# A graph-attention and hypergraph kernel on one core: D^-1 on a path of its own, and a new order of copies, LayerNorm and leaky steps

## The chip, the cores and the metric

The kernel runs on one core of a Trainium2 chip. The metric is the device time of the core in microseconds (us), the median of several runs. Before the change it is 2611.13 us (3 runs, 2609.69 to 2614.38).

In what follows PE is TensorE (matmuls), DVE is VectorE, ACT is ScalarE, POOL is GpSimd and SP is SyncE, which issues nearly all transfers (DMAs). Each engine works through its own instructions in their order and waits for the others by semaphores.

## The reference

There are 128 graphs of 128 nodes with 512 features. Two layers follow each other; each is x = LayerNorm(x + f(x, adj)). Cut to what is computed:

```python
# layer 0: attention with 8 heads of 64 units
feats  = einsum('bnf,hfu->bhnu', X, W)
e_self, e_neigh = feats . a_self, feats . a_neigh
dense  = leaky_relu(e_self[..., :, None] + e_neigh[..., None, :], 0.2)
dense  = dense + -1e10 * (1.0 - A[:, None])
att    = softmax(dense, axis=-1)
x      = layernorm(x + relu(einsum('bhij,bhju->bhiu', att, feats) + b))

# layer 1: two hypergraph convolutions with a ReLU and a LayerNorm between them
H   = (adj != 0);  w = first row of adj
Dn  = 1 / sum_e H[c, e] w[e]      # 0 where the sum is not positive
Be  = 1 / sum_c H[c, e]
conv(x, W, b) = Dn * (H @ (Be * (H^T @ (x W^T)))) + b
x   = layernorm(x + conv(layer_norm(relu(conv(x, W1, b1))), W2, b2) + x)
```

D^-1 in the title is Dn: one number for each node of each graph.

## The kernel before

The kernel takes two graphs ("a pair") at a time, 64 pairs. Each pair goes through several planned periods of T = 38.6 us, and several pairs are in flight. Every step has a planned place, written as (periods after the pair's own start, us within the period). The steps of all pairs are sorted by that time, and this gives the order of the instructions on every engine. The planned times only set the order; nothing waits for a clock.

```python
T = 38.6
for p in range(PAIRS):
    if p > 1:
        todo.append((p * T, load, (p,)))
    if p:
        todo.append((p * T + 19.0, load_blocks, (p,)))
    for lag, time, fn, skip in steps:
        ...
            todo.append(((p + lag) * T + time + shift(p, lag, time), on_pair, (fn, p)))
...
    for _, fn, args in sorted(todo, key=lambda e: e[0]):
        fn(*args)
```

The matrix products are done with a scheme of seven block products in place of eight; it adds several products into one PSUM bank, "X", and needs copies of X between them. For the last dense product of a pair ("py") the products 1, 2, 6, 5, 7, 4, 3 stand at these times, and the copies 0, 1, 2 of X at the last three:

```python
chain("py", 3, (24.2, 29.4, 27.7, 32.9, 31.2, 35.35, 37.1, 26.2, 29.6, 33.1), weigh,
      QU, 1)

def copy(p, s, i):
    ...
    nc.scalar.copy(t[:, :n], s[kind, "X"][:, :n])
```

Product 4 (at 35.35) adds into X again and so has to wait for copy 2 (at 33.1). Product 3 (at 37.1) adds into the bank "W", which a sum on DVE (at 34.9) reads first.

The attention scores start with two small row vectors for each head, e_self and e_neigh. A feature tile ft holds them in its first two columns. The kernel gathers e_neigh, together with D^-1, in a small tile "columns", transposes it, writes it to memory and reads it back spread over all 128 partitions:

```python
@step(0, 11.0)
def nodes(p, s):
    ...                                        # dd = sum of w where adj is not 0
    dn = small.tile([P, 2], F32, tag="dn", name=f"dn_{p}")
    nc.vector.tensor_scalar(dn, dd, TINY, None, op0=ALU.max)
    nc.vector.reciprocal(dn, dn)
    nc.vector.scalar_tensor_tensor(
        columns[p % 2][:, B - CS:B - CS + 2], dd, 0.0, dn, op0=ALU.is_gt, op1=ALU.mult
    )

@step(1, 25.0)
def spread_rows(p, s):
    t = columns[p % 2]
    nc.vector.tensor_copy(
        t[:, B - 2 * H:].rearrange("p (g h) -> p g h", g=2), s["ft"][:, :, :, 1]
    )
    rows = work.tile([P, B], F32, tag="rows", name=f"rows_{p}")
    nc.vector.transpose(rows, t)
    ...
        nc.sync.dma_start(rd.rearrange("b c j -> (b c) j"), rows)

@step(1, 27.0)
def neighbours(p, s):
    s["nb"] = work.tile([P, 2, H * N], F32, tag="nb", name=f"nb_{p}")
    for g in range(2):
        spread(p, s, s["nb"][:, g, :], slice(2 + g * H, 2 + (g + 1) * H))
    s["dnb"] = work.tile([P, 2 * N], F32, tag="dnb", name=f"dnb_{p}")
    spread(p, s, s["dnb"], slice(0, 2))
```

nb then gets the mask (POOL), the leaky step with e_self as its bias (ACT), the maximum (DVE) and the exponential (ACT), for two graphs g and two halves q of the heads. In the loop below tm, tl and tx are the times of mask, leaky step and maximum:

```python
def masked(p, s, g, q):
    ...
    nc.gpsimd.tensor_tensor(
        t, t, neg[:, :, None, :].to_broadcast([P, NB, HH, B]), op=ALU.add
    )

def leaky(p, s, g, q):
    for h in range(q * HH, (q + 1) * HH):
        t = scores(p, s, g, h)
        nc.scalar.activation(t, t, AF.Prelu, bias=s["ft"][:, g, h, 0:1], alpha=SLOPE)

for (g, q), tm, (lag, tl), (lagx, tx), te, tt in (
    ((0, 0), 31.0, (1, 32.4), (1, 33.9), 2.7, 18.1), ((0, 1), 32.2, (1, 34.0), (1, 36.7), 4.6, 18.15),
    ((1, 0), 34.2, (1, 37.5), (2, 2.0), 7.8, 21.5), ((1, 1), 35.4, (2, 6.0), (2, 7.3), 7.9, 21.55),
):
    at(1, tm, masked, g, q)
    at(lag, tl, leaky, g, q)
    ...
```

In the same stretch of a period the pair before is at its first LayerNorm: rstds (a small DVE step "vea" and a power "rsa" on POOL), first_shift ("sh", DVE) and first_output (the scaled and shifted y, ACT). Its y feeds the products "pz", which ACT copies to zT, which feeds the products "ph":

```python
at(2, 32.7, rstds, "a")

@step(2, 34.95)
def first_shift(p, s):
    s["sh"] = small.tile([P, 2], F32, tag="sh", name=f"sh_{p}")
    nc.vector.scalar_tensor_tensor(
        s["sh"], s["mv", "a"][:, :, 0], -1.0, s["rs", "a"], op0=ALU.mult, op1=ALU.mult
    )

def first_output(p, s, g):
    t = s["y"][:, g, :]
    nc.scalar.activation(
        t, t, AF.Identity, bias=s["sh"][:, g:g + 1], scale=s["rs", "a"][:, g:g + 1]
    )

at(2, 35.7, first_output, 0)
at(2, 35.75, first_output, 1)
...
at(3, 0.0, propagate, 0)       # pz
at(3, 0.9, propagate, 1)
...
at(3, 1.1, z_evict, 0)         # zT
at(3, 2.0, z_evict, 1)
```

Two more parts are touched. r_evict multiplies the propagator R by dnb (DVE, at (1, 35.8)). load_blocks loads x and adj in blocks of 32 rows (tiles xb and ab), in four transfers each; ab is used by the step edges at (1, 3.4).

Of the kernel before, what the change touches and what calls it, by code (L numbers as in the profile page):

```python
# [8 lines left out]
F32 = mybir.dt.float32  # L9
AF = mybir.ActivationFunctionType  # L10
ALU = mybir.AluOpType
# [5 lines left out]
TINY = 1.1754944e-38  # L17
# [3 lines left out]
def kernel(  # L21
# [44 lines left out]
    nc = tc.nc  # L66
    G, N, F = x.shape
    P = 128
    DH = w1t.shape[1]
    H = 8  # L70
# [8 lines left out]
    B = 32  # L79
    NB = P // B  # L80

    const = ctx.enter_context(tc.tile_pool(name="const", bufs=1))
    work = ctx.enter_context(tc.tile_pool(name="work", bufs=1))
    small = ctx.enter_context(tc.tile_pool(name="small", bufs=4))
    dram = ctx.enter_context(tc.tile_pool(name="dram", bufs=3, space=bass.MemoryType.DRAM))
# [6 lines left out]
    st = {}  # L92
# [10 lines left out]
    def load_blocks(p):  # L103
        s = st[p]
        gs = slice(2 * p, 2 * p + 2)

        s["xb"] = work.tile([P, 2 * NB, P], F32, tag="xb", name=f"xb_{p}")
        rows = x[gs].rearrange("g (b n) (f c) -> f n (g b) c", b=NB, f=NB)
        for f in range(NB):
            nc.sync.dma_start(s["xb"][f * B:(f + 1) * B], rows[f])  # L110

        s["ab"] = work.tile([P, 2 * NB, B], F32, tag="ab", name=f"ab_{p}")
        rows = adj[gs].rearrange("g (b n) (f e) -> f n (g b) e", b=NB, f=NB)
        for f in range(NB):
            nc.sync.dma_start(s["ab"][f * B:(f + 1) * B], rows[f])

# [15 lines left out]
    for dst, i, j in ((w0_sb[:, 0], 0, 0), (w0_sb[:, 1], 1, 0), (w0_12, 0, 1), (w0_sb[:, 2], 1, 1)):  # L132
        raw = work.tile([P, KF // 2, QU], F32, tag=("eT", "nb", "sq", "hS")[2 * i + j], name=f"w0_raw{i}{j}")
        nc.sync.dma_start(
            raw, w0.rearrange("(p k) c -> p k c", k=KF)
            [:, i * KF // 2:(i + 1) * KF // 2, j * QU:(j + 1) * QU],
        )
        if (i, j) == (1, 0):
            load_blocks(0)
        w0_blocks.append((dst, raw.rearrange("p k (h u) -> p k h u", h=HH), j))  # L140

    def everywhere(ap, n, name):
# [36 lines left out]
    for i in range(2):  # L179
        t = const.tile([P, 2, H, UW + 1], F32, name=f"ft{i}")  # L180
        nc.gpsimd.memset(t[:, :, :, UW:], 1.0)
        fts.append(t)

    CS = 2 + 2 * H
    columns = []
    for i in range(2):
        t = const.tile([P, B], F32, name=f"columns{i}")
        nc.gpsimd.memset(t[:, :B - CS], 0.0)
        columns.append(t)

    def second_sums(eng, w, b12):

# [75 lines left out]
    def step(lag, time, skip_first=False):  # L268
        def keep(fn):
            steps.append((lag, time, fn, skip_first))  # L270
            return fn
        return keep

    def at(lag, time, fn, *args, skip_first=False):
        step(lag, time, skip_first)(lambda p, s: fn(p, s, *args))
# [28 lines left out]
    @step(0, 11.0)  # L304
    def nodes(p, s):

        a = s["a"]
        dd = small.tile([P, 2], F32, tag="dd", name=f"dd_{p}")
        w = s["w"]
        for g in range(2):  # L310
            nc.vector.scalar_tensor_tensor(
                w[:, g, :], a[:, g, :], 0.0, w[:, g, :], op0=ALU.not_equal, op1=ALU.mult,
                accum_out=dd[:, g:g + 1],
            )
        dn = small.tile([P, 2], F32, tag="dn", name=f"dn_{p}")
        nc.vector.tensor_scalar(dn, dd, TINY, None, op0=ALU.max)
        nc.vector.reciprocal(dn, dn)
        nc.vector.scalar_tensor_tensor(
            columns[p % 2][:, B - CS:B - CS + 2], dd, 0.0, dn, op0=ALU.is_gt, op1=ALU.mult
        )  # L320
    @step(0, 38.4)
    def mask(p, s):
        s["neg"] = work.tile([P, 2, N], F32, tag="neg", name=f"neg_{p}", bufs=2)
# [51 lines left out]
    @step(1, 35.8)  # L375
    def r_evict(p, s):
        s["R"] = work.tile([P, 2, N], F32, tag="R", name=f"R_{p}", bufs=3)
        nc.vector.tensor_tensor(
            s["R"].rearrange("p g (b n) -> p g b n", b=NB),
            s["pd"][:, :2 * N].rearrange("p (g b n) -> p g b n", g=2, b=NB),  # L380
            blocked(p, s["dnb"], 2).rearrange("p b g n -> p g b n"), op=ALU.mult,
        )


# [59 lines left out]
    @step(1, 25.0)  # L444
    def spread_rows(p, s):


        t = columns[p % 2]
        nc.vector.tensor_copy(
            t[:, B - 2 * H:].rearrange("p (g h) -> p g h", g=2), s["ft"][:, :, :, 1]  # L450
        )
        rows = work.tile([P, B], F32, tag="rows", name=f"rows_{p}")
        nc.vector.transpose(rows, t)
        shape = [B, NB, B] if p == 0 else [NB, B, B]
        rd = s["rd"] = dram.tile(shape, F32, tag="rd", name=f"rd_{p}")
        if p == 0:
            for b in range(NB):
                nc.sync.dma_start(rd[:, b, :], rows[b * B:(b + 1) * B])
        else:
            nc.sync.dma_start(rd.rearrange("b c j -> (b c) j"), rows)  # L460

    def spread(p, s, dst, rows):

        src = s["rd"]
        rows = slice(B - CS + rows.start, B - CS + rows.stop)
        if p == 0:
            src = src[rows].rearrange("c b j -> (c b j)")
        else:
            dst = dst.rearrange("p (b x) -> p b x", b=NB)
            src = src[:, rows, :].rearrange("b c j -> b (c j)")  # L470
        nc.sync.dma_start(dst, src.partition_broadcast(P))

    def blocked(p, t, n):

        dims = "p (c b j) -> p b c j" if p == 0 else "p (b c j) -> p b c j"
        return t.rearrange(dims, b=NB, c=n)

    @step(1, 27.0)
    def neighbours(p, s):
        s["nb"] = work.tile([P, 2, H * N], F32, tag="nb", name=f"nb_{p}")  # L480
        for g in range(2):
            spread(p, s, s["nb"][:, g, :], slice(2 + g * H, 2 + (g + 1) * H))
        s["dnb"] = work.tile([P, 2 * N], F32, tag="dnb", name=f"dnb_{p}")
        spread(p, s, s["dnb"], slice(0, 2))

    def scores(p, s, g, hs):
        return blocked(p, s["nb"][:, g, :], H)[:, :, hs, :]

# [62 lines left out]
                )  # L553

    for (g, q), tm, (lag, tl), (lagx, tx), te, tt in (
        ((0, 0), 31.0, (1, 32.4), (1, 33.9), 2.7, 18.1), ((0, 1), 32.2, (1, 34.0), (1, 36.7), 4.6, 18.15),
        ((1, 0), 34.2, (1, 37.5), (2, 2.0), 7.8, 21.5), ((1, 1), 35.4, (2, 6.0), (2, 7.3), 7.9, 21.55),
    ):
        at(1, tm, masked, g, q)
        at(lag, tl, leaky, g, q)  # L560
        at(lagx, tx, largest, g, q)
        at(2, te, exponential, g, q)
        at(2, tt, e_transpose, g, q, skip_first=True)
# [64 lines left out]

    at(2, 26.2, residual, 0)
    at(2, 30.7, residual, 1)  # L630
    at(2, 32.7, rstds, "a")

    @step(2, 34.95)
    def first_shift(p, s):
        s["sh"] = small.tile([P, 2], F32, tag="sh", name=f"sh_{p}")
        nc.vector.scalar_tensor_tensor(
            s["sh"], s["mv", "a"][:, :, 0], -1.0, s["rs", "a"], op0=ALU.mult, op1=ALU.mult
        )
# [4 lines left out]
            t, t, AF.Identity, bias=s["sh"][:, g:g + 1], scale=s["rs", "a"][:, g:g + 1]  # L643
        )

    at(2, 35.7, first_output, 0)
    at(2, 35.75, first_output, 1)

    def skip(p, s, g):

# [194 lines left out]
    def o_norm(p, s):  # L845
# [5 lines left out]
    T = 38.6  # L851
    todo = [
        (11.1, prepare_first, (0,)), (12.0, prepare_first, (1,)), (13.0, prepare_first_sums, ()),
        (65.0, prepare_output, ()), (71.4, prepare_output_sums, ()), (73.7, prepare_hidden, (0,)),
        (75.6, prepare_hidden, (1,)), (77.5, prepare_hidden, (2,)), (77.6, prepare_hidden, (3,)),
        (82.0, prepare_output_blocks, ()), (83.0, prepare_output_block_sums, ()),
    ]
# [4 lines left out]
    def shift(p, lag, time):  # L862

        if p == 0:
            if lag == 0:
                return 2.5 if time < 12.0 else 0.0
            if lag == 1 and 4.0 < time < 10.0:
                return -T + (6.8 if time < 6.0 else 8.0)
            if lag == 2 and time < 8.5:
                return -0.8 * time  # L870
        if p == 1 and lag == 1:
            if time < 4.0:
                return -6.0
            return -17.5 if time < 10.0 else -13.0 if time < 12.0 else -23.1 if time < 26.0 else 0.0
        return 0.0

    for p in range(PAIRS):
        if p > 1:
            todo.append((p * T, load, (p,)))
        if p:  # L880
            todo.append((p * T + 19.0, load_blocks, (p,)))
        for lag, time, fn, skip in steps:
            if p or not skip:
                todo.append(((p + lag) * T + time + shift(p, lag, time), on_pair, (fn, p)))
# [47 lines left out]
```

## Time and profile before

| | before |
|---|---|
| median of 3 runs | 2611.13 us |
| span of the profiled run | 2606.9 us |
| mean granted TensorE clock | 0.989 |
| mean DMA rate | 132 GB/s |
| first pz product | 89.6 us after the start |
| first to last pz product | 2469.0 us |

The page gives busy time and share of the span for each engine, and groups of instructions by line, engine and operation with their count and mean duration. "L295" is line 295 of the kernel; a tile's name stands without its buffer number, as in "py<-pyX", which is a copy from the bank X to a tile py. The waits say which engine's instruction stood idle and what ended the idle time. A timeline line has the start and the duration of one piece in us, engine, line, operation, output and inputs, shape, a count, and in brackets the idle time before it and what ended it.

### The profile page before, as it was taken

The numbers are of one execution on the slowest core, as the hardware profiler recorded it, in microseconds if no ns is written. First come the engines' busy times: TensorE is split into PE (matmuls) and PEld (weight loads), VectorE is DVE, ScalarE is ACT, GpSimd is POOL, SyncE is SP. The second block draws the span as 40 slices with busy tenths as digits, with TensorE's granted clock in tenths as the row PEclk, the third lists the DMA queues.
The fourth block names the chain that finished last, engine by engine and source line by source line (L and its number), as shares of the span: only waits on it lengthen the run. The fifth ranks groups of instructions, "written<-read, shape, count | busy, mean of one in ns | idle before, by whom it ended". The sixth has DMA issues, their size and how long they took to land.

```text
span 2606.9 us, 48113 instructions
## 1 busy us (share of the span) xinstructions
PE 2520.7 (97%) x16304; PEld 2274.7 (87%) x16304; DVE 2099.5 (81%) x4648; ACT 1514.9 (58%) x4297; POOL 1724.5 (66%) x1810
## 2 busy tenths in 40 slices
PE   4799999999999999999999999999999999999997
PEld 2798998898898898889899899889889899899986
DVE  5788888888888888888788788788788888888874
ACT  2466566566565565565565565565565565565562
POOL 3566766766666766667667667667667667667653
PEclk8799999999999999999999999999999999999998
DMA  6444544544544544544544544544544544544530
GB/s 164 114 132 130 145 132 137 138 132 131 143 133 126 148 133 130 144 132 128 148 132 124 150 134 125 147 131 127 144 133 131 141 135 131 143 132 131 143 112 22
DMA packets 418649, 344.51 MB, mean 132 GB/s; under 512 B 136930, under 2 KB 367458, under 8 KB 418404
## 3 DMA queue, kind: packets, MB, share of 16 engines
q1 hardware_dynamic: 414708, 340.38, 46.9%
q8 instruction: 130, 2.13, 0.3%
q10 hardware_dynamic: 3696, 1.06, 0.2%
q14 instruction: 115, 0.94, 0.1%
HBM read 240.66 MB, written 100.67 MB: 131 GB/s over the span
## 4 chain that ended last, share of the span: by engine, by line
PE 79%; DMA 11%; DVE 3%; ACT 2%; issue 2%; POOL 2%; SPq 0%; DVEq 0%; ACTq 0%; POOLq 0%
PE phX L700 18%; PE pyX L414 10%; PE pfX L414 9%; PE phW L700 9%; DMA nb<-rd 8%; PE pyW L414 6%; PE pav L574 6%; PE pz L665 4%; PE phY L700 4%; PE pfW L414 4%; PE pq L824 4%; DMA rd<-rows 2%; PE pfY L414 2%; PE pyY L414 2%; ACT nb L501 2%
## 5 line engine op out<-in xcount | busy, mean ns | idle before, releaser
L501 ACT ACTIVATE nb<-nb,ft 128x128 f32<-128x128 f32 x1024 | 326.5, 392 | 285.7 <-POOL nb L494 220.6
L494 POOL TENSOR_TENSOR nb<-nb,neg 128x512 f32<-128x512 f32 x256 | 321.0, 1276 | 136.0 <-DMA nb<-rd 89.8
L700 PEld LDWEIGHTS phX<-zS,w_sb 128*128 128x128 f32 x3072 | 363.0, 192 | 31.2 <-issue 31.2
L700 PE MATMUL phX<-zS,w_sb 128*128 128x128 f32 x3072 | 374.2, 275 | 0.7 <-issue 0.7
L751 POOL TENSOR_TENSOR sq<-sq 128x512 f32<-128x512 f32 (+2 forms) x384 | 343.0, 893 | 41.8 <-ACT sq L740 21.7
L515 ACT ACTIVATE nb<-nb,nm 128x128 f32<-128x128 f32 x1024 | 320.3, 393 | 0.7 <-DVE nm L507 0.7
L507 DVE TENSOR_REDUCE nm<-nb 128x4 f32<-128x512 f32 x256 | 174.3, 681 | 142.9 <-ACT nb L501 88.8
L295 ACT COPY py<-pyX 128x257 f32<-128x257 f32 (+1 forms) x192 | 70.5, 367 | 360.3 <-PE pyX L414 354.8
L414 PE MATMUL pyX<-w_sb,h 128*128 128x257 f32 (+1 forms) x1024 | 250.1, 386 | 18.3 <-ACT py L295 17.2
L621 POOL TENSOR_TENSOR rso<-veo,mhalf 128x2 f32<-128x2 f32 x64 | 44.9, 701 | 332.0 <-DVE veo L619 322.0
L574 PEld LDWEIGHTS pav<-ft,eT 128*128 128x128 f32 x2048 | 251.6, 194 | 11.5 <-DVE eT L536 3.4
L414 PE MATMUL pyX<-w_sb,hS 128*128 128x257 f32 (+1 forms) x1024 | 248.2, 384 | 5.0 <-POOL hS L396 5.0
L574 PE MATMUL pav<-ft,eT 128*128 128x65 f32 x2048 | 246.2, 274 | 3.2 <-DVE eT L536 3.2
L730 ACT ACTIVATE h<-h,b_sb 128x128 f32<-128x128 f32 x768 | 239.5, 392 | 5.7 <-DVE h L715 5.6
L414 PE MATMUL pyW<-w_sb,hS 128*128 128x256 f32 x1024 | 242.3, 378 | 0.0
L414 PEld LDWEIGHTS pyX<-w_sb,h 128*128 128x128 f32 x1024 | 190.0, 191 | 56.3 <-ACT py L295 30.7
L605 DVE SCALAR_TENSOR_TENSOR y<-y,x 128x512 f32<-128x512 f32 x128 | 145.8, 1139 | 95.7 <-POOL y L598 95.7
L598 POOL TENSOR_TENSOR y<-y,b_bc 128x512 f32<-128x512 f32 x128 | 162.5, 1269 | 89.4 <-DVE y L589 89.4
L414 PEld LDWEIGHTS pyW<-w_sb,hS 128*128 128x128 f32 x1024 | 193.7, 189 | 27.8
L414 PEld LDWEIGHTS pyX<-w_sb,hS 128*128 128x128 f32 x1024 | 190.2, 191 | 30.5 <-POOL hS L396 5.4
L396 POOL TENSOR_TENSOR xS<-xT 128x256 f32<-128x256 f32 x128 | 121.6, 950 | 89.2 <-DVE xT L334 85.8
L295 ACT COPY ph<-phX 128x512 f32<-128x512 f32 x192 | 112.6, 586 | 93.8 <-PE phX L700 89.3
(121 smaller groups left out, 5821.7 us busy)
## 6 DMA issues: line engine op xcount, KB each, us to landing
nb<-rd SPq DMA_DIRECT2D x128, 512.0 KB, 6.0
ed<-nb SPq DMA_DIRECT2D x126, 512.0 KB, 3.1
eb<-ed SPq DMA_DIRECT2D x504, 128.0 KB, 2.8
xb<-in_x_dram SPq DMA_DIRECT2D x256, 128.0 KB, 3.6
x<-in_x_dram SPq DMA_DIRECT2D x64, 512.0 KB, 9.3
out_dram<-o SPq DMA_DIRECT2D x64, 512.0 KB, 3.2
a<-in_adj_dram SPq DMA_DIRECT2D x64, 128.0 KB, 8.0
w<-in_adj_dram SPq DMA_DIRECT2D x128, 64.0 KB, 6.9
```

What stands on the lines that cost most here:

```text
L295: nc.scalar.copy(t[:, :n], s[kind, "X"][:, :n])
L414: nc.tensor.matmul(to[:, :n], lhs[:, k, :], rhs[:, k, :n], start=bool(start) and k == 0, stop=(k == nk - 1), skip_group_check=True,)
L494: nc.gpsimd.tensor_tensor(t, t, neg[:, :, None, :].to_broadcast([P, NB, HH, B]), op=ALU.add)
L501: nc.scalar.activation(t, t, AF.Prelu, bias=s["ft"][:, g, h, 0:1], alpha=SLOPE)
L507: nc.vector.tensor_reduce(s["nm"][:, g, hs], scores(p, s, g, hs).rearrange("p b h j -> p h b j"), AX.XY, ALU.max, negate=True,)
L515: nc.scalar.activation(t, t, AF.Exp, bias=s["nm"][:, g, h:h + 1])
L574: nc.tensor.matmul(t[:, h * (U + 1):(h + 1) * (U + 1)], s["eT"][:, g, q * HH + h, :], s["ft"][:, g, q * HH + h, 2:], start=True, stop=True,)
L598: nc.gpsimd.tensor_tensor(s["y"][:, g, :], s["y"][:, g, :], b0_bc, op=ALU.add)
L605: nc.vector.scalar_tensor_tensor(y, y, 0.0, s["x"][:, g, :], op0=ALU.max, op1=ALU.add)
L700: nc.tensor.matmul(to[:, m * N:(m + 1) * N], w[:, k, m * P:(m + 1) * P], rhs[:, k, :], start=bool(start) and m == 0 and k == 0, stop=(k == ...
L730: nc.scalar.activation(dst[:, k, :], src[:, k, :], AF.Relu, bias=b1_sb[:, c:c + 1])
L751: nc.gpsimd.tensor_tensor(t[:, :n, :], t[:, :n, :], t[:, n:2 * n, :], op=ALU.add)
```

## The change

D^-1 leaves the path of the scores. It is transposed alone in the step nodes, written to memory by itself (write_nodes) and read back spread (spread_nodes), so that nothing of it has to stand beside e_neigh. The scores are then transposed straight from ft, without the tile columns and the copy into it. The blocks of adj are loaded behind the spreads and no longer with those of x. Three times in the plan move: the leaky steps of the first graph go from 32.4 and 34.0 to 33.2 and 35.0, behind the third copy of X (33.1); the LayerNorm's rstds, first_shift and first_output go from 32.7, 34.95, 35.7 and 35.75 to 31.5, 33.0, 34.5 and 34.55, so that they stand behind the first mask and the first leaky steps instead of behind two of each. No matmul is added, removed or moved.

The diff, cut where it only renames:

```diff
+    def load_edges(p):
+        s = st[p]
         s["ab"] = work.tile([P, 2 * NB, B], F32, tag="ab", name=f"ab_{p}")
...
         if (i, j) == (1, 0):
             load_blocks(0)
+            load_edges(0)
...
-    CS = 2 + 2 * H
-    columns = []
-    for i in range(2):
-        t = const.tile([P, B], F32, name=f"columns{i}")
-        nc.gpsimd.memset(t[:, :B - CS], 0.0)
-        columns.append(t)
+    dn = const.tile([P, B], F32, name="dn")
+    nc.gpsimd.memset(dn, 0.0)
...
-        dn = small.tile([P, 2], F32, tag="dn", name=f"dn_{p}")
-        nc.vector.tensor_scalar(dn, dd, TINY, None, op0=ALU.max)
-        nc.vector.reciprocal(dn, dn)
-        nc.vector.scalar_tensor_tensor(
-            columns[p % 2][:, B - CS:B - CS + 2], dd, 0.0, dn, op0=ALU.is_gt, op1=ALU.mult
-        )
+        t = dn[:, :2]
+        nc.vector.tensor_scalar(t, dd, TINY, None, op0=ALU.max)
+        nc.vector.reciprocal(t, t)
+        nc.vector.scalar_tensor_tensor(t, dd, 0.0, t, op0=ALU.is_gt, op1=ALU.mult)
+        s["dr"] = work.tile([P, B], F32, tag="dr", name=f"dr_{p}")
+        nc.vector.transpose(s["dr"], dn)
+
+    @step(0, 17.0)
+    def write_nodes(p, s):
+        s["dd"] = dram.tile([NB, B, B], F32, tag="dd", name=f"dd_d_{p}")
+        nc.sync.dma_start(s["dd"].rearrange("b c n -> (b c) n"), s["dr"])
...
-        t = columns[p % 2]
-        nc.vector.tensor_copy(
-            t[:, B - 2 * H:].rearrange("p (g h) -> p g h", g=2), s["ft"][:, :, :, 1]
-        )
         rows = work.tile([P, B], F32, tag="rows", name=f"rows_{p}")
-        nc.vector.transpose(rows, t)
+        nc.vector.transpose(
+            rows.rearrange("p (c x) -> p c x", c=2),
+            s["ft"][:, :, :, :2].rearrange("p g h c -> p c (g h)"),
+        )
...
+    @step(1, 28.0)
+    def spread_nodes(p, s):
+        s["dnb"] = work.tile([P, NB, 2, B], F32, tag="dnb", name=f"dnb_{p}")
+        nc.sync.dma_start(
+            s["dnb"].rearrange("p b g n -> p b (g n)"),
+            s["dd"][:, :2, :].rearrange("b g n -> b (g n)").partition_broadcast(P),
+        )
...
-        ((0, 0), 31.0, (1, 32.4), (1, 33.9), 2.7, 18.1), ((0, 1), 32.2, (1, 34.0), (1, 36.7), 4.6, 18.15),
+        ((0, 0), 31.0, (1, 33.2), (1, 33.9), 2.7, 18.1), ((0, 1), 32.2, (1, 35.0), (1, 36.7), 4.6, 18.15),
...
-    at(2, 32.7, rstds, "a")
-    @step(2, 34.95)
+    at(2, 31.5, rstds, "a")
+    @step(2, 33.0)
     def first_shift(p, s):
...
-    at(2, 35.7, first_output, 0)
-    at(2, 35.75, first_output, 1)
+    at(2, 34.5, first_output, 0)
+    at(2, 34.55, first_output, 1)
...
         if p:
             todo.append((p * T + 19.0, load_blocks, (p,)))
+            todo.append((p * T + 28.5, load_edges, (p,)))
```

More of the change, by code (lines that the diff above doesn't have):

```diff
@@ L110, in load_blocks @@
             nc.sync.dma_start(s["xb"][f * B:(f + 1) * B], rows[f])
+    def load_edges(p):
+        s = st[p]
         s["ab"] = work.tile([P, 2 * NB, B], F32, tag="ab", name=f"ab_{p}")
-        rows = adj[gs].rearrange("g (b n) (f e) -> f n (g b) e", b=NB, f=NB)
+        rows = adj[2 * p:2 * p + 2].rearrange("g (b n) (f e) -> f n (g b) e", b=NB, f=NB)
         for f in range(NB):
@@ L380, in r_evict @@
             s["pd"][:, :2 * N].rearrange("p (g b n) -> p g b n", g=2, b=NB),
-            blocked(p, s["dnb"], 2).rearrange("p b g n -> p g b n"), op=ALU.mult,
+            s["dnb"].rearrange("p b g n -> p g b n"), op=ALU.mult,
         )
@@ L445, in spread_rows @@
     def spread_rows(p, s):
-        t = columns[p % 2]
-        nc.vector.tensor_copy(
-            t[:, B - 2 * H:].rearrange("p (g h) -> p g h", g=2), s["ft"][:, :, :, 1]
-        )
-        rows = work.tile([P, B], F32, tag="rows", name=f"rows_{p}")
-        nc.vector.transpose(rows, t)
+        rows = work.tile([P, B], F32, tag="rows", name=f"rows_{p}")
+        nc.vector.transpose(
+            rows.rearrange("p (c x) -> p c x", c=2),
+            s["ft"][:, :, :, :2].rearrange("p g h c -> p c (g h)"),
+        )
         shape = [B, NB, B] if p == 0 else [NB, B, B]
@@ L460, in spread_rows, with blocked @@
             nc.sync.dma_start(rd.rearrange("b c j -> (b c) j"), rows)
[L462 to L476, printed above, removed]
+    def blocked(p, t):
+        dims = "p (h b j) -> p b h j" if p == 0 else "p (b h j) -> p b h j"
+        return t.rearrange(dims, b=NB, h=H)
     @step(1, 27.0)
@@ L481, in neighbours @@
         for g in range(2):
-            spread(p, s, s["nb"][:, g, :], slice(2 + g * H, 2 + (g + 1) * H))
-        s["dnb"] = work.tile([P, 2 * N], F32, tag="dnb", name=f"dnb_{p}")
-        spread(p, s, s["dnb"], slice(0, 2))
+            dst, src, hs = s["nb"][:, g, :], s["rd"], slice((2 + g) * H, (3 + g) * H)
+            if p == 0:
+                src = src[hs].rearrange("h b j -> (h b j)")
+            else:
+                dst = dst.rearrange("p (b x) -> p b x", b=NB)
+                src = src[:, hs, :].rearrange("b h j -> b (h j)")
+            nc.sync.dma_start(dst, src.partition_broadcast(P))
+    @step(1, 28.0)
[5 more added lines that the diff above has]
+        )
     def scores(p, s, g, hs):
-        return blocked(p, s["nb"][:, g, :], H)[:, :, hs, :]
+        return blocked(p, s["nb"][:, g, :])[:, :, hs, :]
     def masked(p, s, g, q):
```

## The prediction

> **What bounds the kernel now.** I read the page's first part, then the waits, then the timelines of one stage engine by engine.
>
> ```profile
> PE 2520.7 (97%) x16304; PEld 2274.7 (87%) x16304; DVE 2099.5 (81%) x4648; ACT 1514.9 (58%) x4297; POOL 1724.5 (66%) x1810
> ```
>
> TensorE (PE) is the bound: 97% busy, and no other engine is near it. The change takes no matmul away, so all it can win is time in which PE stands still. The waits of all engines, cut to two lines (total us, times, longest), say which wait that is in the steady part:
>
> ```profile
> POOL nb L494 <- DMA nb<-rd: 89.8, 58, 2.9
> ...
> PE pyX L414 <- ACT py L295: 17.2, 34, 1.3
> ```
>
> The timeline of PE around one pair shows where it sits:
>
> ```profile
> 1022.19 1.89 PE L414 MATMUL pyX<-w_sb,hS 128*128 128x256 f32 x8
> ...
> 1026.09 0.38 PE L794 MATMUL pm<-ident,sq 128*128 128x128 f32 x2
> 1027.44 2.00 PE L414 MATMUL pyX<-w_sb,h 128*128 128x256 f32 x8 [0.97 <-ACT py L295]
> 1029.28 1.89 PE L414 MATMUL pyW<-w_sb,hS 128*128 128x256 f32 x8
> 1031.01 1.95 PE L665 MATMUL pz<-R,y 128*128 128x128 f32 x16
> 1032.79 2.00 PE L700 MATMUL phX<-zT,w_sb 128*128 128x128 f32 x16
> ```
>
> PE stops once per pair, after pm: the next product adds into bank X, and ScalarE's copy of X has not been made. To size it I took start-to-start times from the trace, since the modelled ends hide part of a gap. The 64 first pz starts give 61 steady spacings (the first, 41.07 us, and the last, 37.15 us, left out): least 38.67 us, median 39.11, mean 39.19. Of 59 of these I took each group of matmuls apart: every group keeps its time within 0.1 us, except pm, which takes 0.22 to 1.72 us and is 25.6 us over its 0.22 in sum, and the pyX behind it, 5.2 us over (0.10 us each time PE has stood). So all steady loss is at one place, 31 us in 59 pairs, about 32 us in 61.
>
> Why is the copy late? ScalarE (ACT) in the same stage:
>
> ```profile
> 1025.86 1.28 ACT L501 ACTIVATE nb<-nb,ft 128x128 f32<-128x128 f32 x4 [4.79 <-DMA nb<-rd]
> 1027.04 0.35 ACT L295 COPY py<-pyX 128x256 f32<-128x256 f32 x1
> 1027.29 1.28 ACT L501 ACTIVATE nb<-nb,ft 128x128 f32<-128x128 f32 x4
> 1029.00 1.52 ACT L642 ACTIVATE y<-y,sh,rsa 128x512 f32<-128x512 f32 x2 [0.43 <-DVE sh L636]
> 1030.43 0.35 ACT L781 COPY y<-pyX 128x256 f32<-128x256 f32 x1
> 1030.68 1.28 ACT L501 ACTIVATE nb<-nb,ft 128x128 f32<-128x128 f32 x4
> 1032.10 0.59 ACT L677 COPY zT<-pz 128x512 f32<-128x512 f32 x1
> ```
>
> X was complete near 1024.1 (1022.19 + 1.89), yet the copy runs at 1027.04: it stands in the in-order queue behind four leaky steps, which wait for the first mask on GpSimd (POOL), which waits for the neighbour scores to land:
>
> ```profile
> 1024.55 2.51 POOL L494 TENSOR_TENSOR nb<-nb,neg 128x512 f32<-128x512 f32 x2 [2.80 <-DMA nb<-rd]
> 1027.01 0.71 POOL L621 TENSOR_TENSOR rsa<-vea,mhalf 128x2 f32<-128x2 f32 x1
> 1027.68 2.51 POOL L494 TENSOR_TENSOR nb<-nb,neg 128x512 f32<-128x512 f32 x2
> ```
>
> Call the start of the first mask M, counted from the start of pm. Over 57 pairs the stall is M + 2.67 us to 0.01 us, or nothing where that is negative (here M = -1.54, stall 1.13). M runs from -3.07 to -1.17, usually near -2.3. The chain is DMA, POOL, ACT, PE; PE is held by a transfer through a copy that doesn't need it.
>
> **What the Trainium skill says.** "SBUF — State Buffer", section "Who interferes with whom": a VectorE copy in a two-port mode, or a VectorE instruction with two SBUF inputs, contends with GpSimd, and "Whoever issues first gets the shared pair for the whole instruction; the other fully blocks". The trace agrees, on two small VectorE (DVE) instructions of this change:
>
> ```profile
> 1015.91 0.72 DVE L449 COPY columns<-ft 128x16 f32<-128x16 f32 x1
> 1016.67 0.21 DVE L453 STREAM_TRANSPOSE rows<-columns 128x32 f32<-128x32 f32 x1
> ...
> 1028.15 0.82 DVE L636 SCALAR_TENSOR_TENSOR sh<-mva,rsa 128x2 f32<-128x2 f32 x1
> ```
>
> The copy has a minimum of 171 ns and a median of 716; sh 152 and 812, and here it ends at 1028.97, when the third mask (1027.68 plus half of 2.51) ends. The transpose takes 211 to 214 ns every time. "DMA: Bandwidth & Descriptors", section "Queues, rings and completion order", says that an engine consumes one ring's descriptors in order. The packets agree: dnb is issued 6.8 us before pm, and its 256-byte packets start 3 us before it, when about 600 of the 1,024 packets of nb have started.
>
> **The change part by part.**
> 1. *Copy of columns removed, scores transposed straight from ft.* From the start of the copy to that of the transpose are 0.75 us in the median (0.24 to 1.18). The strided read may cost a little. The row write, the spread and so M come about 0.7 us earlier: M near -3.0.
> 2. *D^-1 transposed alone and written by itself.* One DVE transpose more (64 x 0.21 = 13.5 us in all), one copy less (46.5 us in all): DVE is relieved. One 16 KB write more per pair, landing in about 1.4 us as the row write does. By the planned times in the source, (0, 17.0) and (1, 28.0) at a period of 38.6, it comes 49.6 us ahead of its reader. No PE time.
> 3. *adj blocks behind the spreads.* The 1,024 packets of 128 bytes per pair now run mostly 12 to 10 us before pm, and DMA is nearly idle (0.02 to 0.15 of its engines) when the spread is issued. So nothing was in its way: gain about 0. They now fill 1.9 us of issue time behind dnb, and are used 7.0 us after pm (L347); there is slack. x, a and w come some 2 us later, and are used later still.
> 4. *Third copy of py ahead of the leaky step.* It runs when X is complete, near pm - 1.9, for 0.35 us. The 32 us stall as it stands is gone.
> 5. *LayerNorm around the masks.* POOL now does one mask, rsa, then three; ACT does leaky, y (L642), leaky. A new chain follows M: mask 1.23, rsa 0.67, sh; the second mask starts with sh and blocks it, 1.25 + 0.05; two y 1.43, leaky 1.19, the copy of py to y2 0.26, leaky 1.19. ACT is free for zT at M + 7.3. Without a stall pz starts at pm + 3.69, and zT starts 1.08 later in the trace, pm + 4.77. The limit is M = -2.5. Likewise DVE does sh, then nm, then the sum of pyW, ending at M + 4.25; the second pyW product overwrites that bank at pm + 1.96: M = -2.4 at most.
>
> With M 0.7 to 0.75 earlier, the new limit is passed only in pairs whose present stall is over 0.9 us: eight of 57, by 0.02 to 0.6 us, in sum 2 to 3 us with the restarts.
>
> Sum: 2611.1 - 32 + 3 = 2582; I say 2583. At both ends I expect nothing: the first pz, at 89.6 us, waits for the LayerNorm of pair 0, where sh already is blocked by a mask (1.21 us) and that order brings no more.
>
> **The rivals.**
> *The wait moves.* If the strided transpose is as slow as the copy was, M stays at -2.3, and with the limit -2.5 most pairs stall again at phX (waiting for zT): about 0.25 us each, some 17 to 20 us, a time near 2598. For it: the new order puts rsa ahead of one mask only, and a mask blocks sh. Against it: no transposition in this trace shows a block.
> *The transfer gets slower.* The small adj packets, and x behind them, could slow nb itself: 0.5 us in M less gained leaves M near -2.55 and a sum of some 10 us, near 2590. Against it is the order in the ring.
> *Another engine becomes the bound.* In 40 us DVE works 32 to 34 and POOL 27 to 28; at a period of 38.67 neither is full. If it came, 39.2 again, 2611.
> *PE itself gets no faster.* 38.67 us is its own pace, so 61 x 38.67 and the two ends are the floor: near 2579.
>
> **Range and chances.** Floor 2579, central 2583, rivals up to 2600. The 2% line is 2559, below the floor, so a verdict of faster would need a gain that I can't see at the ends of the run or in PE's pace; slower by 2% would need a new wait of over 0.8 us per pair.
>
> **What would show it.** Step 1: no line for columns; the transpose near 0.21 us; the row write is issued 9.9 us before pm instead of 9.18. Step 4: "PE pyX <- ACT py" gone from the waits, ACT's three copies of py in a row. Step 5: sh near 1.2 us, and a small wait of phX for zT or pyW for y. Sum: median spacing of pz 38.7 us. The prediction is wrong if the spacing stays at 39 or more, if the spread lands later, or if PE stalls at a place I haven't named.

## The result, and the profile after

| | before | after |
|---|---|---|
| median | 2613.97 us (6 runs) | 2590.4 us (6 runs, 2585.7 to 2590.82) |
| ratio to before, with its 95% interval | | 0.9908 [0.9895, 0.9921] |
| span of the profiled run | 2606.9 us | 2587.2 us |
| start of the first pz | 89.6 us | 92.9 us |
| spacing of pz, first / mean of the 61 that follow / least of these | 41.07 / 39.19 / 38.67 us | 39.69 / 38.84 / 38.67 us |

The change is 0.9% faster; the medians differ by 23.6 us, the two profiled runs, which are single executions, by 19.7 us of span. These 19.7 us add up so: the 61 steady periods are 21.5 us shorter, the first pz comes 3.3 us later, the first spacing is 1.4 us shorter, and the end gives 0.1 us.

The page of the changed kernel has TensorE (PE) at the same share, with 7.6 us less of busy time (PEld are its weight loads):

```profile
PE 2513.1 (97%) x16304; PEld 2271.3 (88%) x16304; DVE 2137.3 (83%) x4648; ACT 1516.3 (59%) x4297; POOL 1721.5 (67%) x1809
```

More telling is the chain of work that ended last, by engine, here of the kernel before:

```profile
PE 79%; DMA 11%; DVE 3%; ACT 2%; issue 2%; POOL 2%; SPq 0%; DVEq 0%; ACTq 0%; POOLq 0%
```

and of the changed kernel:

```profile
PE 91%; DMA 4%; DVE 2%; issue 1%; POOL 1%; ACT 0%; SPq 0%; ACTq 0%; POOLq 0%; DVEq 0%
```

The chain through the spread of the scores (DMA) is mostly gone, but not wholly. In the waits of PE the line of pyX on the ACT copy of py is gone; a shorter one stands in its place (total us, times, longest):

```profile
PE pyW L418 <- DVE y L788: 3.5, 9, 1.0
```

The timeline of PE in a pair whose scores land late shows the new place:

```profile
1253.15 0.38 PE L799 MATMUL pm<-ident,sq 128*128 128x128 f32 x2
1253.37 1.90 PE L418 MATMUL pyX<-w_sb,h 128*128 128x256 f32 x8
1256.27 2.00 PE L418 MATMUL pyW<-w_sb,hS 128*128 128x256 f32 x8 [1.01 <-DVE y L788]
1258.11 1.95 PE L670 MATMUL pz<-R,y 128*128 128x128 f32 x16
```

pyX now follows pm at once (0.22 us), and PE stands one product later, ahead of pyW. The same pair on ACT:

```profile
1251.23 0.37 ACT L294 COPY py<-pyX 128x256 f32<-128x256 f32 x1 [3.10 <-PE pyX L418]
1253.41 1.28 ACT L506 ACTIVATE nb<-nb,ft 128x128 f32<-128x128 f32 x4 [1.81 <-POOL nb L499]
1255.33 1.52 ACT L647 ACTIVATE y<-y,sh,rsa 128x512 f32<-128x512 f32 x2 [0.64 <-DVE sh L641]
1256.75 1.26 ACT L506 ACTIVATE nb<-nb,ft 128x128 f32<-128x128 f32 x4
```

The copy waits for PE alone, 1.9 us before pm; the leaky steps and y come behind it. On POOL:

```profile
1252.11 1.27 POOL L499 TENSOR_TENSOR nb<-nb,neg 128x512 f32<-128x512 f32 x1 [3.33 <-DMA nb<-rd]
1253.34 0.70 POOL L626 TENSOR_TENSOR rsa<-vea,mhalf 128x2 f32<-128x2 f32 x1
1254.01 3.73 POOL L499 TENSOR_TENSOR nb<-nb,neg 128x512 f32<-128x512 f32 x3
```

and on DVE:

```profile
1254.07 1.22 DVE L641 SCALAR_TENSOR_TENSOR sh<-mva,rsa 128x2 f32<-128x2 f32 x1 [3.23 <-POOL rsa L626]
1255.21 0.67 DVE L512 TENSOR_REDUCE nm<-nb 128x4 f32<-128x512 f32 x1
1255.81 0.40 DVE L788 TENSOR_TENSOR y<-py,pyW 128x256 f32<-128x256 f32 x1
```

This is the chain that step 5 of the prediction wrote down: one mask, rsa, then sh, which starts 0.06 us behind the second mask and takes 1.22 us instead of 0.16, then nm, then the sum that frees the bank of pyW.

### The profile page after: what moved, and what is told of

It is laid out like the page before. It is cut to its first block, busy times and chain, and to the rows that moved or that the text cites. A ratio compares the mean times of both kernels' runs of the same rounds, so it can differ in the third digit from the quotient of the medians.

```text
span 2587.2 us, 48238 instructions
## 1 busy us (share of the span) xinstructions
PE 2513.1 (97%) x16304; PEld 2271.3 (88%) x16304; DVE 2137.3 (83%) x4648; ACT 1516.3 (59%) x4297; POOL 1721.5 (67%) x1809
## 4 chain that ended last, share of the span: by engine, by line
PE 91%; DMA 4%; DVE 2%; issue 1%; POOL 1%; ACT 0%; SPq 0%; ACTq 0%; POOLq 0%; DVEq 0%
PE phX L705 18%; PE pyX L418 15%; PE pfX L418 9%; PE phW L705 9%; PE pyW L418 8%; PE pav L579 8%; PE phY L705 4%; PE pz L670 4%; PE pfW L418 4%; PE pq L829 4%; PE pyY L418 4%; PE pfY L418 2%; DMA nb<-rd 2%; PE pd L374 1%; DMA rd<-rows 1%
## 5 line engine op out<-in xcount | busy, mean ns | idle before, releaser
L756 POOL TENSOR_TENSOR sq<-sq 128x512 f32<-128x512 f32 (+2 forms) x384 | 342.3, 891 | 29.6 <-ACT sq L745 8.6
L506 ACT ACTIVATE nb<-nb,ft 128x128 f32<-128x128 f32 x1024 | 325.4, 390 | 39.1 <-POOL nb L499 34.5
L610 DVE SCALAR_TENSOR_TENSOR y<-y,x 128x512 f32<-128x512 f32 x128 | 154.6, 1208 | 133.2 <-POOL y L603 132.9
L418 PE MATMUL pyX<-w_sb,h 128*128 128x257 f32 (+1 forms) x1024 | 244.3, 381 | 0.0
```

The costliest lines, as they stand in the source:

```text
L418: nc.tensor.matmul(to[:, :n], lhs[:, k, :], rhs[:, k, :n], start=bool(start) and k == 0, stop=(k == nk - 1), skip_group_check=True,)
L610: nc.vector.scalar_tensor_tensor(y, y, 0.0, s["x"][:, g, :], op0=ALU.max, op1=ALU.add)
L756: nc.gpsimd.tensor_tensor(t[:, :n, :], t[:, :n, :], t[:, n:2 * n, :], op=ALU.add)
```

## The experiments

One table for all of them. M is, as in the prediction, the start of the first mask from the start of pm, here the mean over the same 57 pairs. The stall is what the stretch from pm to pq takes in these pairs over 14.45 us, its least in all kernels but g1, in sum. L is the offset in "stall = M + L", the median over the pairs that stall. The spread is the time of the first nb transfer from its issue to its landing, in the mean (its standard error is 0.03 to 0.07 us; L is taken over pairs with a stall of over 0.15 us). Ratios are to runs of the kernel before on the same chip.

| kernel | ratio [95%] | M, us | L, us | stall, us | spread, us |
|---|---|---|---|---|---|
| before | 1 | -2.28 | 2.77 | 29.6 | 5.32 |
| c1_copy: copy ahead of leaky | 0.9968 [0.9956, 0.9980] | -2.14 | 2.52 | 22.9 | 5.29 |
| c2_norm: LayerNorm order | 0.9997 [0.9987, 1.0007] | -2.27 | 2.78 | 29.4 | 5.29 |
| c3_path: D^-1 path and transpose | 0.9981 [0.9973, 0.9989] | -2.46 | 2.77 | 25.7 | 5.65 |
| f2_copy_ab: c1 and adj blocks behind | 0.9938 [0.9925, 0.9950] | -2.19 | 2.51 | 19.3 | 5.21 |
| **after** | 0.9908 [0.9895, 0.9921] | -2.60 | 2.45 | 10.0 | 5.62 |
| d2_norm_back: after, LayerNorm undone | 0.9905 [0.9892, 0.9919] | -2.49 | 2.51 | 12.0 | 5.76 |
| d1_ab_back: after, adj blocks undone | 0.9975 [0.9965, 0.9985] | -2.12 | 2.45 | 27.4 | 5.76 |
| e1_own_dn: after, transpose undone | 1.0107 [1.0092, 1.0121] | -1.39 | 2.45 | 64.6 | 5.82 |
| c4_dr2: after, two buffers for dr | 0.9900 [0.9887, 0.9914] | -2.49 | 2.48 | 12.8 | 5.73 |
| d3_sum_first: c4 and the sum first | 0.9909 [0.9896, 0.9923] | -2.57 | 2.46 | 11.0 | 5.72 |
| **d4_after_zt**: d3 and leaky behind zT | **0.9842** [0.9829, 0.9855] | -2.43 | none | 0.3 | 5.82 |
| f1_extra_write: before and a write | 0.9982 [0.9975, 0.9989] | -2.30 | 2.77 | 27.6 | 5.23 |
| g1_dnb_early: after, D^-1 read early | 1.0521 [1.0496, 1.0547] | -0.06 | 2.44 | 147.8 | 5.26 |

M, L, stall and spread come from one execution of each kernel. That of the kernel before took 2608.7 us, 5 us under the median of the six runs above; that of c1 took 2609.1 us, the longest of its six. So a difference of a few us between two stalls of the table is not by itself an effect of an edit; the ratios rest on all runs.

**The copy by itself.**

```diff
-        ((0, 0), 31.0, (1, 32.4), ...), ((0, 1), 32.2, (1, 34.0), ...),
+        ((0, 0), 31.0, (1, 33.2), ...), ((0, 1), 32.2, (1, 35.0), ...),
```

> The kernel before with one edit: the leaky steps of the first graph stand behind the third copy of X. Theory (the chain nb, mask, leaky, copy holds PE): the gap behind pm is gone. M, the start of the first mask, stays at -2.3 us from pm, as the row write is not touched. With rsa still behind two masks, ACT is free for zT at M + 7.33, against pm + 4.82 at the latest, so PE now waits before ph (zT) where M is over -2.5: by the M of the trace before, 15.9 us in 57 pairs instead of 24, and the sum of pyW on DVE ends at M + 3.65 and holds nothing. Time about 13 us under before, 2601. Rival A (the copy was the only limit, no second one close behind): 31 us less, 2583. Rival B (the change's gain came from the earlier row write): no gain, 2614.

2606.08 us: 8 us less, not 13 and not 31. L fell from 2.77 to 2.52 as worked out from the trace before, and PE's wait went where it was expected:

```profile
PE phX L700 <- ACT zT L677: 10.0, 29, 0.6
```

M was 0.14 us later, which the expectation had not foreseen, and in some eight pairs products of pf took longer, 4.8 us in sum. In one of these, at 267 us, pfX starts 0.1 us after the end of ACT's copy of pf, and that copy starts 0.4 us after its bank was complete, behind activations of h; why ACT is late there stays open. So the most visible wait was worth a quarter of its 32 us, because a second one stood 0.25 us behind it.

**LayerNorm's order by itself, and taken back.** The times of rstds, first_shift and first_output, in the kernel before (c2) and undone in the changed kernel (d2):

```diff
-    at(2, 32.7, rstds, "a")            # d2: the other way round
-    @step(2, 34.95)
-    at(2, 35.7, first_output, 0)
+    at(2, 31.5, rstds, "a")
+    @step(2, 33.0)
+    at(2, 34.5, first_output, 0)
```

> The kernel before with one edit: rstds, first_shift and first_output at the earlier times, so that rsa stands behind one mask and not two. Theory: PE still waits for the third copy of X, which stands behind the first leaky steps, at M + 2.67; the order of LayerNorm isn't on that chain. No gain: 2614, within 3 us. Rival: LayerNorm's y is what pz waits for, and an earlier y gives some 10 us.

2614.35 us, no difference. PE still waits for the copy, as the waits of this kernel show:

```profile
PE pyX L414 <- ACT py L295: 16.7, 29, 1.2
```

> The changed kernel with LayerNorm's three steps back at the times before, so that rsa stands behind two masks. Theory: where PE stalls, the whole stall of a pair is M + 2.77 in the kernel before, M + 2.52 with the copy alone moved, and M + 2.45 in the changed kernel: the LayerNorm order adds nothing to the copy's, it only moves the place of the wait from ph (zT) to pyW (the sum on DVE). Expected: the place moves back to ph, the time stays, 2590 within 3 us. Rival: the parts are worth more together, as the copy alone gave 8 us, the path alone 6 and both with LayerNorm 24; then this loses 5 to 10 us, 2595 to 2600.

2594.23 us beside 2619.26 on that chip: 0.9905, the changed kernel's ratio within 0.0003. The wait moves from pyW back to ph:

```profile
PE phX L705 <- ACT zT L682: 4.3, 14, 0.4
```

The new order makes y early, but y is not what is late. It makes the sum of pyW later, as a mask blocks sh, and L is 2.45 us with it and 2.51 without. Its own worth can't be told from nil in either place; the intervals leave some 3 us in c2 and 5 us in d2.

**The path by itself.** The changed kernel with the old order and the adj blocks beside x:

```diff
-            todo.append((p * T + 28.5, load_edges, (p,)))
+            todo.append((p * T + 19.0, load_edges, (p,)))
```

(and the leaky and LayerNorm times of the kernel before).

> The changed kernel with its order undone: D^-1 on its own path and scores transposed from ft, but adj blocks with those of x, leaky steps and LayerNorm at the times before. The row write is issued 9.9 us before pm instead of 9.18. Theory 1 (the spread takes as long as before, 5.3 us from issue to landing; in the changed kernel the adj blocks behind it made it 5.7): M moves by 0.7 to -3.0, the stall M + 2.67 falls from 24 to some 4 us in 57 pairs, 22 us gained, less 3 us at the start for the single buffer of dr: 2594. Theory 2 (an earlier spread simply lands less than that earlier, whatever is behind it): M is -2.6 as in the changed kernel, the stall 14 us, 2602 to 2606.

2608.11 us, 0.9981. The row write was issued at -9.91 us (median), but the first spread took 5.65 us instead of 5.32: theory 2. M moved by 0.2 us, and the stall fell by 3.9 us. How much of the 6 us comes from the earlier scores is not shown: f1 below has only an extra write, with scores as late as before, and gains as much (0.9982).

**The adj blocks.** The diff above alone, in the changed kernel:

> The changed kernel with the adj blocks back among the loads with x. Theory: the blocks have no part in it; the first spread lands 5.65 us after its issue as in the changed kernel and in the path alone, M stays near -2.5, 2590 within 3 us. Rival 1: behind the spread they slow it; taken away, M goes to -3.0 and the time to 2583. Rival 2: ahead of it they slow it, as the path alone had M at -2.46 against -2.60; then M -2.4, 2593.

2613.79 us, 0.9975: neither the theory nor rival 1. The blocks are worth 0.9975 - 0.9908, or 17 us (give or take 4, by the two intervals), and rival 2 had only the direction. The spread is hardly longer than in other kernels of its kind, but it starts late. SP's queue in this kernel:

```profile
1018.61 2.34 SPq L110 DMA_DIRECT2D xb<-in_x_dram  x4
1020.99 1.94 SPq L118 DMA_DIRECT2D ab<-in_adj_dram  x4
1023.93 0.34 SPq L463 DMA_DIRECT2D rd<-rows  x1
1025.37 0.94 SPq L480 DMA_DIRECT2D nb<-rd  x2
```

Here ab is issued until 1 us before the row write. Over the pairs the last of the 1,024 packets of these blocks starts 8.9 us before pm in the mean, behind the issue of the row write; in the kernel before it started at -9.5, ahead of the row write at -9.2. The write, due at -9.9, is issued at -9.65 in the mean and takes 1.67 us to land instead of 1.53, the spread is issued at -8.00 instead of -8.37 and takes 0.14 us longer, and M is in the end 0.48 us later. The write of D^-1 (0.47 us of issue time) stands ahead of x, and the write of the scores comes 0.7 us earlier: the two have closed the gap that was there before. No run takes the two apart.

The queue alone does not fix the cost. c3 has the same order of transfers, but there the transfer of the results at their head (out_dram) is issued at -16.2 us in the mean, in d1 at -15.8; c3 issues its row write at -9.84 and has M at -2.46. Why the head of the queue comes later in d1 stays open.

The other test of the blocks is on the kernel before, with the copy moved (c1) and the blocks behind the spreads:

> The kernel before with two edits: the leaky steps behind the third copy of X, and the adj blocks behind the spreads. Theory: the blocks were in nobody's way as long as the row write comes at -9.2 us from pm; it is the earlier write (and the write of D^-1 ahead of the x blocks) that meets them. So nothing is gained over the copy order alone (2606, 0.9968): 0.9965 to 0.9975. Rival: the blocks cost the spread something there too, M moves by 0.2 us or more, and the time falls by 8 us or more, to 0.994 or less.

2599.42 us, 0.9938: 8 us less than the copy alone (give or take 4 to 5), so the rival holds in its size. M moved by 0.05 us only; the stall fell by 3.6 us, and the 4.8 us in the products of pf were gone. By which path the blocks make this gain, and what links those products to them, is not shown.

**The copy of the scores kept.** In the changed kernel:

```diff
-        nc.vector.transpose(rows.rearrange(...), s["ft"][:, :, :, :2].rearrange(...))
+        t = columns[p % 2]
+        nc.vector.tensor_copy(t[:, B - 2 * H:].rearrange(...), s["ft"][:, :, :, 1])
+        nc.vector.transpose(rows, t)
```

> The changed kernel with the scores copied to a small tile before their transpose, as in the kernel before, while D^-1 keeps its own path. The row write is issued 9.2 us before pm again. If the landing of the spread depends on the time of the write (it got 0.35 us longer as the write came 0.72 earlier), the first spread takes 5.3 us again and M is -2.3, with a stall M + 2.45 of 14 us in 57 pairs: 2594. If instead the separate memory of D^-1, or its own read, makes the spread longer, it takes 5.65 us with the late write as well: M near -1.95, stall some 28 us, 2608.

2646.35 us, 1.0107, worse than either theory. The tile's view shows the reason (min/median/max in ns):

```profile
L459 DVE COPY columns<-ft x64: 163/1178/1235, 42.5 to 2545.3; 128x16 f32<-128x16 f32 x64
L462 DVE STREAM_TRANSPOSE rows<-columns x64: 210/211/214, 42.7 to 2546.0; 128x32 f32<-128x32 f32 x64
```

The copy meets the same POOL operation as in the kernel before, y<-y,b_bc of 1.27 us (in 55 of the 57 pairs here, in 53 there), but it starts 0.12 us after that operation and not 0.59, and in both kernels it ends with it: it takes 1.18 us, not 0.72. The write comes at -8.77 us in the mean. The spread takes 5.82 us although the write is late, so its length doesn't depend on the time of the write. In means, the spread is issued at -7.33, lands 5.8 us later, and the mask starts 0.14 us after that: -1.39, the measured M. The transpose from ft takes 0.22 to 0.24 us in all 64 pairs of the changed kernel; without it the other parts of the change lose time.

**The start.** In the changed kernel:

```diff
-        s["dr"] = work.tile([P, B], F32, tag="dr", name=f"dr_{p}")
+        s["dr"] = work.tile([P, B], F32, tag="dr", name=f"dr_{p}", bufs=2)
```

> The changed kernel with two buffers for dr. Theory: the 3.3 us by which the first pz came later in the changed kernel (92.9 against 89.6 us) are from DVE, which waits 4.75 us at 39.5 us for the write of pair 0's dr before it can transpose that of pair 1. With two buffers that wait is gone and the first pz is back near 90: 2587 against 2590. Rival: the transfers in front of it on SP's queue are what is late (the adj blocks, the extra write), DVE then waits for xb or ab instead, and the first pz stays near 93.

The first pz is at 87.9 us. The wait for dr was this line of the changed kernel's tile view (us, times):

```profile
  DVE dr L319: 4.8, 1
```

and it is gone. In time, 0.9900 and 0.9908 can't be told apart; the steady stall happened to be 2.8 us larger in this profile.

**Both limits behind the mask.** First the sum of pyW ahead of sh (with two buffers for dr):

```diff
-    at(3, 34.9, y_sum, 1, 1, 2, "W")
+    at(3, 33.15, y_sum, 1, 1, 2, "W")
-    @step(2, 33.0)
+    @step(2, 33.17)
     def first_shift(p, s):
```

> The changed kernel with two buffers for dr and the DVE sum of pyW ahead of sh and nm, but the leaky step of graph 1 still ahead of the zT copies. Theory: there are two limits of nearly the same size behind the mask; without the wait for the sum PE reaches pz earlier, and the copy of zT comes no earlier, so the wait moves to ph: total stall M + 2.5 as before, 10 to 13 us, and a ratio near 0.990. Rival: the sum was the limit by itself, and 8 us are gained, 0.987.

2590.92 us, 0.9909, nothing gained. The wait for the sum became the wait for zT, as expected:

```profile
PE phX L705 <- ACT zT L682: 7.8, 18, 1.1
```

Then also the leaky step of graph 1 behind the zT copies, with the first exponentials (2.7 to 4.1) and one maximum (2.0 to 5.35) moved back to fit:

```diff
-        ((0, 0), 31.0, (1, 33.2), (1, 33.9), 2.7, 18.1), ...
-        ((1, 0), 34.2, (1, 37.5), (2, 2.0), 7.8, 21.5), ...
+        ((0, 0), 31.0, (1, 33.2), (1, 33.9), 4.1, 18.1), ...
+        ((1, 0), 34.2, (2, 2.3), (2, 5.35), 7.8, 21.5), ...
```

> The changed kernel with four edits that take both places of the remaining stall off the chain behind the mask: dr has two buffers; DVE sums pyW ahead of sh and nm; the leaky step of graph 1 stands behind both zT copies and not ahead of them, with the first exponentials behind the copy of ph; nm of graph 1 behind the transposes of x. Theory: the remaining stall (10 us in 57 pairs, 13 with two buffers for dr) is all from these two places; zT is then held only where M is over -1.3, pyW never. The spacing of pz goes to 38.7 in nearly every pair, 8 to 12 us under the changed kernel: 2579. Rival: the late exponentials or the late maximum hold PE at a later place (the copies of ph, xS for pf), and nothing is gained or the time goes up: 2590 or more.

2577.92 us beside 2619.26: **0.9842**, 1.6% under the kernel before and faster than the changed one by 0.0066, 17 us. The mean spacing of pz is 38.71 us, and the chain that ended last is PE nearly throughout:

```profile
PE 96%; DVE 1%; DMA 1%; issue 1%; POOL 0%; ACT 0%; SPq 0%; POOLq 0%; DVEq 0%; ACTq 0%
```

The scores land as late as ever (M = -2.43), and PE no longer waits for what hangs on them: 0.3 us of stall in 57 pairs. The move of the leaky step without the sum ahead of sh was not run.

**Why the spread takes longer.** First the kernel before with a write of zeros at the place of D^-1's write:

```diff
+    @step(0, 17.0)
+    def write_nodes(p, s):
+        s["dd"] = dram.tile([NB, B, B], F32, tag="dd", name=f"dd_d_{p}")
+        nc.sync.dma_start(s["dd"].rearrange("b c n -> (b c) n"), dn0)
```

> The kernel before with one addition: at the place of the changed kernel's write of D^-1, a tile of zeros of the same size is written to a memory of its own that nothing reads; D^-1 still travels with the scores. In all six kernels with D^-1 on its own path the first spread takes 5.6 to 5.8 us from issue to landing, in the three without it 5.3. Theory 1 (the extra write and its memory are the cause): 5.65 us here too, and with M later, about 16 us more: 2630. Theory 2 (D^-1 read from a memory of its own is the cause, or the row of D^-1 missing beside the scores): 5.3 us, time 2614, or a few us more if the write pushes the blocks behind it into the row write.

The spread takes 5.23 us: it isn't the write. The time was 0.9982, 5 us less; why an extra write should help is not shown, and its stall (27.6 us) is near that of before.

Then the changed kernel with D^-1 read ahead of the x blocks:

```diff
-    @step(1, 28.0)
+    @step(1, 18.5)
     def spread_nodes(p, s):
```

> The changed kernel with the read of D^-1 issued ahead of the x blocks, some 15 us before pm, instead of behind the spreads of the scores; nothing else moves. The first spread took 5.25 us in the kernel before with an extra write, so the write of D^-1 is not what makes it 5.6 to 5.8; left are its read, running beside the spread, and the layout of the rows. Theory (the read beside it): with the read out of the way the first spread takes 5.3 us, M goes to -3.0 and the stall from 10 us to some 4 in 57 pairs: 2583, 0.988. Rival 1 (the rows, or something not named): 5.65 us still, M near -2.6, 0.991. Rival 2: the 512 packets ahead of the x blocks push these into the row write, M comes later, 0.993 or more.

The spread takes 5.26 us, with the new rows and the extra write in place: what is left, and goes with the longer time, is the read of D^-1 from a memory of its own behind the spreads. This kernel differs in much else (M, the stall), so the test is not free of rivals; the new rows with D^-1 read from the memory of the scores were not run. The kernel is also 5% slower, rival 2 with much more force than expected. The read's own line (us from issue to landing, min/median/max):

```profile
DMA to landing us min/median/max: 4.7/6.6/8.0
```

Between 13 and 11 us before pm the 16 engines start 117 to 127 of its 256-byte packets per us and are busy 14 to 15% of the time, while the x blocks wait behind them in the queue. The row write behind these lands 4.4 us after its issue instead of 1.4, and M is -0.06.

## Why the prediction was right or wrong, point by point

*What bounds the kernel* was right. All the steady loss of the changed kernel is again behind the first mask, and the floor of 38.67 us per pair is the least spacing in it too.

*Step 1* was right up to the spread: the transpose from ft takes 0.24 us in the median, the row write is issued at -9.91 us as predicted. "M near -3.0" was wrong. It is -2.60 in the mean: the row write came 0.73 us earlier, but the spread got 0.3 us longer, a time that the prediction had taken as fixed, and the write 0.07. This is the term of the sum that was mis-sized: the stall left over was put at 2 to 3 us and is 10.0 in 57 pairs.

*Step 2*, "no PE time", was wrong at the start: with one buffer for dr, DVE stands 4.8 us once for a write that is deep in SP's queue. *"At both ends I expect nothing"* fails for the same reason; the first pz came 3.3 us later. And D^-1's path is not free in the steady part: its read goes with the longer spread (g1). "DVE is relieved" did not hold for the change as a whole: DVE's busy time rose from 2099.5 to 2137.3 us. By the medians of sh (0.81 and 1.22 us, 64 times) about 26 us of that are sh, which the second mask now blocks in full. DVE is not the bound, so this cost nothing beyond the chain of step 5.

*Step 3*, "gain about 0", was wrong. It was read from the kernel before, where the last packet of the blocks started ahead of the row write. It did not ask what step 1 and the new write do to that gap. Given the other parts the blocks are worth 17 us (d1), and 8 us even with the late write (f2). That the time still came out near the prediction is luck in this point: the change happened to contain the move that the prediction held to be worth nothing, and without it the same sum would have been forecast for d1, which gains 0.25%.

*Step 4* was right in mechanism: ACT's three copies wait for PE alone, the third runs 1.92 us before pm in all 57 pairs, and the gap behind pm is gone in each.

*Step 5* was right. The limit was put at M = -2.5 for zT and -2.4 for pyW (the terms it gives for pyW, 1.96 - 4.25, make -2.3); measured, a pair begins to stall at -2.55, and the pyW wait sets in at -2.2. The prediction listed LayerNorm's order without a gain, and c2 and d2 show none.

*The sum*: 2583 us from 2611, a ratio of 0.989, against 0.9908 [0.9895, 0.9921]. Two errors pull the same way: M, with 10 us of stall in place of 3, and the start, with 3.3 us. With these and the first spacing, 1.4 us shorter, the same sum gives 2591. The median spacing is 38.80 us, not 38.7. The rival "the transfer gets slower", put at M = -2.55, some 10 us of stall and 2590, is what came true, though not for the reason it gave: neither adj nor x packets slow the spread, as f2 has the blocks behind it and takes 5.21 us, and the kernel before has x behind it and takes 5.32.

## What to carry to other kernels

When one engine is the bound and waits once per round, work out how far behind the next-latest dependency stands before counting the gap as gain: here 32 us of gap gave 8, as another wait stood 0.25 us behind it, and the rest came only when M moved and, in d4, when everything that hung on the late transfer had been ordered behind what PE needs. On an in-order queue it is not the late operation that has to be faster, but the one that doesn't need it that has to stand in front. And a gap in a DMA queue that is free today is not free once the same change makes the next transfer earlier and puts another in front.

## What the hardware showed that was not expected

The first spread (512 KB) took 5.2 to 5.3 us in six kernels and 5.6 to 5.8 us in the eight in which D^-1 is read from another memory right behind it, while the second spread landed earlier in the latter (6.9 to 7.2 us from its issue, against 7.2 to 8.3). The packets of the first spread start at nearly the same rate in both: the 512th packet of nb starts 4.3 to 4.4 us after the issue in the kernel before and in the changed one. Why a later read from elsewhere delays the first spread and not the second stays open.

A read of 128 KB in 512 packets of 256 bytes, spread from 1 KB, held up the transfers behind it in the queue, so that the row write landed 3 us later (4.4 us from its issue against 1.4), though the DMA engines were busy only 14 to 15% of the time between 13 and 11 us before pm, while its packets ran.
